# A 17-tap convolution in a graph kernel, computed through Fourier components along the nodes

## The chip, the cores and the metric

One core of one Trainium2 chip runs the whole program. The metric is the device time of one execution in microseconds (us), the median of several. "Clock" is the share of full speed that the throttle granted to TensorE. A ratio is the mean time of one kernel's fast runs over the mean time of the other's fast runs of the same rounds, so it is not quite the ratio of the medians quoted beside it.

## The reference, cut to what matters

128 graphs of 128 nodes with 256 channels, in float32. Layer 0 is a gated update whose input comes from a convolution along the nodes and from a weighted sum over neighbours. Layer 1 is a small graph convolution on the first 25 nodes.

```python
def _L0_gnn_ref(x, mask, w_se, b_se, conv1_w, ..., conv2_w, ...):
    xc = jnp.transpose(x, (0, 2, 1))
    h = _bn(_conv1d(xc, conv1_w, 0), bn1_g, bn1_b, bn1_m, bn1_v)
    h = jax.nn.relu(h)
    h = _bn(_conv1d(h, conv2_w, 8), bn2_g, bn2_b, bn2_m, bn2_v)   # 17 taps, 256 -> 256 channels
    x_conv = jnp.transpose(jax.nn.relu(h + xc), (0, 2, 1))
    ...                                    # x_nmp: exp(-dist) * mask times relu(x @ w_msg.T)
    x_in = jnp.concatenate([x_conv, x_nmp], axis=-1)
    gi = x_in @ w_ih.T + b_ih
    gh = x @ w_hh.T + b_hh
    ...                                    # gates r, z, n
    return (1.0 - z) * nn_ + z * x
```

## The kernel before

The graphs go through in 32 passes of four (4 x 128 nodes = 512 columns). Everything stays in SBUF: a pass normalises, transposes and applies the first convolution (`front`), computes the 17-tap convolution (`conv2`), the neighbour sum and the gates (`gru`). After every four passes one block of layer 1 is interleaved with the next passes (`block`).

```python
    def conv2(q, between):
        xc = fr.tile([P, 2, 512], FP, tag="xc", name=f"xc{q}")
        src = h1p[q % 2]                                   # [128, 2, 4 graphs, 128 + 16 nodes]
        for co in range(2):
            pc = pacc.tile([P, 512], FP, tag="acc", name=f"p2{q}_{co}")
            i = 0
            for k in range(2):
                for t in range(TAPS):
                    nc.tensor.matmul(pc.rearrange("p (j n) -> p j n", j=GB),
                                     c2w[:, k, t, co * P:(co + 1) * P], src[:, k, :, t:t + N],
                                     start=(i == 0), stop=(i == 2 * TAPS - 1))
                    i += 1
            ...                                            # batch norm, residual, relu
            if co == 0:
                between()                                  # a piece of layer 1, then neighbours(q)
        return xc
    # ... cut ...
    for q in range(NQ):
        xc = conv2(q, between)
        if q + 1 < NQ:
            front(q + 1)
        gru(q, xc)
        # ... loads, and block(q // QS) after every fourth pass
```

## Time and profile before

| before | value | how to read it |
|---|---|---|
| time | 3819.15 us (3818.87 to 3821.99, 3 runs) | the spread is 0.1% |
| matmuls of `conv2` | 2176 of 512 columns, 1911 us busy of the 3674 us of TensorE | half of the kernel |
| DMA | 57 MB, 15 GB/s in the mean | the queues are busy in the first slice alone |

The prediction shows the lines that carry this. Two more lines of the page matter for the comparison: TensorE's granted clock in 40 slices of the span, in tenths, and the DMA total.

```profile
PEclk9999999999999999999999999999999999999996
DMA packets 62287, 56.84 MB, mean 15 GB/s; under 512 B 7381, under 2 KB 59738, under 8 KB 61914
```

TensorE runs at full clock everywhere but in the last slice, and the memory system is idle.

### The profile page before, as it was taken

The page shows a single profiled execution, that of the slowest core. Times are in us where ns is not written, and L with a number is a line of the kernel's source. Part 1 is how long each engine was busy: PE and PEld are TensorE (multiplying, and loading weights), DVE is VectorE, ACT ScalarE, POOL GpSimd, SP SyncE. Part 2 cuts the span into 40 slices and gives each one's busy share as a digit, 9 for nine tenths or more (in the row PEclk, how much of TensorE's full clock was granted, in tenths as well). Part 3 has the DMA queues.
Part 4 walks back from the last instruction along what each step waited for, and adds up shares of the span by engine and source line. Part 5 has one row for each costly group of instructions (what it writes and reads, how often), then busy time and mean ns, then how long its engine had stood idle before and what let it go on. Part 6 is the DMA issues. An engine that isn't in the chain of part 4 may idle for free.

```text
span 3818.0 us, 25995 instructions
## 1 busy us (share of the span) xinstructions
PE 3673.6 (96%) x10930; PEld 1828.5 (48%) x10930; DVE 605.0 (16%) x1370; ACT 544.2 (14%) x833; POOL 392.2 (10%) x536
## 2 busy tenths in 40 slices
PE   5999999999999999999999999999999999999997
PEld 2444445544445544555445554445544455444454
DVE  1111121111111111111211112111121111211112
ACT  0111110111111111111111111111111111111111
POOL 1010010101101011000110001000010100110000
PEclk9999999999999999999999999999999999999996
DMA  4000000000000000000000000000000000000000
GB/s 155 10 13 13 3 13 13 13 10 18 4 13 13 13 15 12 4 13 13 16 13 3 13 13 18 10 13 3 13 18 13 10 7 9 19 13 10 7 5 11
DMA packets 62287, 56.84 MB, mean 15 GB/s; under 512 B 7381, under 2 KB 59738, under 8 KB 61914
## 3 DMA queue, kind: packets, MB, share of 16 engines
q1 hardware_dynamic: 55808, 41.97, 4.1%
q10 hardware_dynamic: 6362, 13.22, 1.0%
q8 instruction: 85, 1.39, 0.1%
q14 instruction: 32, 0.26, 0.0%
HBM read 38.38 MB, written 16.78 MB: 14 GB/s over the span
## 4 chain that ended last, share of the span: by engine, by line
PE 94%; POOL 2%; ACT 1%; DMA 1%; DVE 1%; issue 0%; ACTq 0%; POOLq 0%; SPq 0%; DVEq 0%
PE p L316 47%; PE pz L342 9%; PE pr L342 9%; PE pn L342 6%; PE pc L250 3%; PE pm L295 3%; PE pg L342 3%; PE ph L452 3%; PE pz L458 3%; PE px L303 2%; PE pse L259 1%; POOL d L363 1%; POOL go L365 1%; PE pg L477 1%; PE pd L273 1%; PE po L378 1%
## 5 line engine op out<-in xcount | busy, mean ns | idle before, releaser
L316 PE MATMUL p<-h1p,c2w 128*128 128x512 f32 x4352 | 1911.1, 592 | 0.0
L316 PEld LDWEIGHTS p<-h1p,c2w 128*128 128x128 f32 x4352 | 809.8, 188 | 962.1 <-issue 956.8
L362 POOL TENSOR_TENSOR d<-hT,r 128x512 f32<-128x512 f32 x64 | 82.5, 1288 | 2014.7 <-ACT r L355 2014.7
L320 DVE SCALAR_TENSOR_TENSOR xc<-p,s_bn,hT 128x512 f32<-128x512 f32 x64 | 48.1, 751 | 1228.7 <-PE p L316 1228.7
L243 ACT ACTIVATE hT<-ph 128x512 f32<-128x512 f32 x64 | 37.9, 592 | 794.4 <-PE ph L241 794.4
L454 ACT ACTIVATE hh<-ph,vec 128x96 f32<-128x96 f32 (+3 forms) x160 | 61.9, 399 | 556.6 <-PE ph L452 551.5
L351 DVE SCALAR_TENSOR_TENSOR r<-pg,vec,r 128x512 f32<-128x512 f32 x64 | 48.0, 751 | 544.5 <-PE pg L342 503.9
L250 PE MATMUL pc<-hT,c1w 128*128 128x512 f32 x256 | 120.2, 613 | 7.7 <-ACT hT L243 7.7
L285 POOL TENSOR_TENSOR b<-adj,cst 25x12 f32<-25x12 f32 (+4 forms) x256 | 52.5, 235 | 671.8 <-DMA adj<-in_adj 556.7
L295 PE MATMUL pm<-wmsg,hT 128*128 128x256 f32 x512 | 121.1, 379 | 0.0
L322 ACT ACTIVATE xc<-xc,t_bn 128x512 f32<-128x512 f32 x64 | 45.8, 716 | 526.4 <-DVE xc L320 526.4
L342 PE MATMUL pr<-hT,whh 128*128 128x512 f32 x256 | 120.3, 592 | 0.0
L342 PE MATMUL pz<-hT,whh 128*128 128x512 f32 x256 | 120.3, 592 | 0.0
L342 PE MATMUL pz<-xnmp,wih 128*128 128x512 f32 x256 | 120.3, 592 | 0.0
L342 PE MATMUL pg<-hT,whh 128*128 128x512 f32 x256 | 120.3, 592 | 0.0
L342 PE MATMUL pz<-xc,wih 128*128 128x512 f32 x256 | 120.3, 592 | 0.0
L342 PE MATMUL pn<-xnmp,wih 128*128 128x512 f32 x256 | 120.3, 592 | 0.0
L342 PE MATMUL pr<-xnmp,wih 128*128 128x512 f32 x256 | 120.3, 592 | 0.0
L342 PE MATMUL pn<-xc,wih 128*128 128x512 f32 x256 | 120.3, 592 | 0.0
L342 PE MATMUL pr<-xc,wih 128*128 128x512 f32 x256 | 120.3, 592 | 0.0
L452 PE MATMUL ph<-yz,w 128*128 128x96 f32 (+3 forms) x640 | 109.0, 323 | 0.5 <-DVE yz L444 0.5
L458 PE MATMUL pz<-hh,w 128*128 128x96 f32 (+3 forms) x640 | 108.3, 322 | 0.0
(121 smaller groups left out, 2663.2 us busy)
## 6 DMA issues: line engine op xcount, KB each, us to landing
xt<-in_x SPq DMA_DIRECT2D x128, 128.0 KB, 2.7
out<-xt SPq DMA_DIRECT2D x128, 96.0 KB, 1.9
adj<-in_adj SPq DMA_DIRECT2D x32, 256.0 KB, 2.8
w<-in_W ACTq DMA_DIRECT2D x2, 2560.0 KB, 15.6
c2w<-in_conv_w ACTq DMA_DIRECT2D x2, 2176.0 KB, 12.9
out<-x SPq DMA_DIRECT2D x128, 32.0 KB, 1.6
wih<-in_w_ih ACTq DMA_DIRECT2D x1, 1536.0 KB, 11.2
whh<-in_w_hh ACTq DMA_DIRECT2D x1, 768.0 KB, 13.7
```

The source lines that it names most:

```text
L250: nc.tensor.matmul(pc, c1w[:, k, co * P:(co + 1) * P], hT[:, k], start=(k == 0), stop=(k == 1))
L285: nc.gpsimd.tensor_tensor(b1[:, b0:b0 + GB, r:r + w], ad[:NN, :, n:n + w], ident[:NN, None, n:n + w].to_broadcast([NN, GB, w]), ALU.add)
L295: nc.tensor.matmul(pm[:, i], hT[:, k, j * N:(j + 1) * N], wmsg[:, k], start=(k == 0), stop=(k == 1))
L303: nc.tensor.matmul(px[:, dc, i], msg[:, i, dc * P:(dc + 1) * P], aT[:, 2 * h + i], start=True, stop=True)
L316: nc.tensor.matmul(pc.rearrange("p (j n) -> p j n", j=GB), c2w[:, k, t, co * P:(co + 1) * P], src[:, k, :, t:t + N], start=(i == 0), stop= ...
L320: nc.vector.scalar_tensor_tensor(xc[:, co], pc, scl["bn2"][:, co:co + 1], HT[q][:, co], op0=ALU.mult, op1=ALU.add)
L342: nc.tensor.matmul(ps, w, a, start=(i == 0), stop=(i == len(ops) - 1))
L351: nc.vector.scalar_tensor_tensor(r, ph, v("b_hh", 4 + dc), r, op0=ALU.add, op1=ALU.mult)
L362: nc.gpsimd.tensor_sub(d, hT[:, dc], r)
L452: nc.tensor.matmul(ph, w1[:, g, k, m * P:(m + 1) * P], yz[:, k, :, o:o + n], start=(k == 0), stop=(k == 1))
L454: nc.scalar.activation(hh[:, m], ph, AF.Relu, bias=v("b1", g * 4 + m))
L458: nc.tensor.matmul(pz, w2[:, g, m, cc * P:(cc + 1) * P], hh[:, m], start=(m == 0), stop=(m == 3))
```

## The change

A convolution along the nodes is a product, component by component, in a Fourier basis along the nodes. With length 136 = 128 + 8 the wrapped ends don't reach the nodes that are kept. 17 multiply passes become a forward transform, one complex product for each component and an inverse transform. A component's product needs all graphs at once to fill TensorE (128 graphs are the rows of its output), so the work becomes three stages with DRAM between them. Stage 1 is 32 passes of `front` and neighbours, each with its forward transform; among them stand eight chunks that transform the taps and store them (`wd`). Stage 2 multiplies component by component. Stage 3 is the inverse transform, the gates and layer 1. The core of the diff, with cuts:

```diff
-    def conv2(q, between):
-        ...                                   # 68 matmuls of 512 columns in a pass
+    def first_stage(es):
+        ...                                   # front(q), back(q): as before, outputs stored to DRAM
+            for k in range(2):                # forward transform of a pass
+                pf = p2.tile([P, 2, 2 * D], FP, tag="b2", name=f"pf{q}_{k}")
+                for h in range(2):
+                    for i in range(2):
+                        nc.tensor.matmul(pf[:, h, i * NC:(i + 1) * NC],
+                                         H1[q, h][:, i, k * P:(k + 1) * P], c("fh"), ...)
+        TC = 8
+        def taps(ch):
+            wt = fa.tile([P, TC, D], FP, tag="wt", name=f"wt{ch}")
+            for i in range(4):                # 17 taps in each of four groups of 32 rows
+                nc.sync.dma_start(out=wt[i * 32:i * 32 + 16], in_=src[:16])
+                nc.sync.dma_start(out=wt[i * 32 + 16:i * 32 + TAPS], in_=src[16:])
+            for j in range(TC // 2):
+                for i in range(4):            # 16 products: 17 rows, 128 components, 512 columns
+                    pw = p1.tile([P, 512], FP, tag="t", name=f"pw{ch}_{j}_{i}")
+                    nc.tensor.matmul(pw, fw[i * 32:i * 32 + TAPS, :P], rows(i, j), ...)
+                    ws = fa.tile([P, 512], FP, tag="ws", name=f"ws{ch}_{j}_{i}", bufs=3)
+                    ...                       # ScalarE or VectorE: ws <- pw
+                    nc.sync.dma_start(out=wd[:P, ...], in_=ws)              # 256 KB
+            for i in range(4):                # 16 narrow products: the other 8 components
+                pw = p1.tile([P, 512], FP, tag="t", name=f"pwt{ch}_{i}")
+                for j in range(TC // 2):
+                    nc.tensor.matmul(pw[j * WIDE:(j + 1) * WIDE],
+                                     fw[i * 32:i * 32 + TAPS, P:P + WIDE], rows(i, j), ...)
+                ...                           # ws (tag "wst", one buffer) <- pw, four small stores
+        for q in range(NQ):
+            ...                               # front(q), back(q - 1)
+            if q % 3 == 1 and q // 3 < n_chunks:
+                taps(q // 3)
+    def second_stage(es):
+        for b in range(NC // 4):              # 34 blocks of four components
+            wt = sb.tile([P, 4, 2 * D], FP, tag="wt", name=f"wf{b}", bufs=3)
+            nc.sync.dma_start(out=wt, in_=wd[4 * b:4 * b + 4]...)           # 1 MB
+            ...                               # wm = wi - wr, wp = wr + wi; xs = xr + xi
+            ...                               # k1 = xs wr, k2 = xr wm, k3 = xi wp: 12 matmuls of 256
+            nc.vector.tensor_add(yy[:, :, 1], s, ks[1])
+            nc.vector.tensor_sub(yy[:, :, 0], s, ks[2])
+            nc.scalar.dma_start(out=to, in_=yt)                             # 0.5 MB
+    def inverse(q):                           # stage 3: 2 matmuls of 512, 8 of 128 columns
+        ...
```

## The prediction

> **What bounds the kernel now.** I read the page first (busy shares, slices), then the chain that ended last, then the groups of instructions kept apart by shape, and last the timeline of one pass and of the tail.
>
> ```profile
> PE 3673.6 (96%) x10930; PEld 1828.5 (48%) x10930; DVE 605.0 (16%) x1370; ACT 544.2 (14%) x833; POOL 392.2 (10%) x536
> PE   5999999999999999999999999999999999999997
> DMA  4000000000000000000000000000000000000000
> ```
>
> TensorE works without a gap from the second slice on, the other engines are at 16% or less, and the DMA queues matter in the first slice alone. So TensorE's columns are the time. Groups and chain say which:
>
> ```profile
> L316 PE MATMUL p<-h1p,c2w 128*128 128x512 f32 x4352 | 1911.1, 592 | 0.0
> L342 PE MATMUL pr<-hT,whh 128*128 128x512 f32 x256 | 120.3, 592 | 0.0
> L303 PE MATMUL px<-aT,msg 128*128 128x128 f32 x512 | 69.5, 279 | 0.0
> L483 PE MATMUL pf<-zt,s2w 128*64 128x256 f32 x128 | 24.6, 468 | 12.5 <-ACT zt L480 12.5
> ...
> 162.23 27.55 PE p L316 x64
> 199.91 25.83 PE p L316 x60
> 267.63 27.55 PE p L316 x64
> ```
>
> L316, the 17-tap convolution, has 4352 records for 2176 matmuls, two records each. 64 records take 27.55 us, so a record takes 430.5 ns and a matmul of 512 columns 861 ns: 1.68 ns a column. One group of four graphs (a pass; 32 of them) holds 68 such matmuls, 58.5 us; from 162.23 to 267.63 a pass without layer 1 takes 105.4 us. The durations that I use below come from the timeline:
>
> ```profile
> 1398.53 0.87 PE L378 MATMUL po<-cst,go 128*128 128x128 f32 x6 [1.54 <-POOL go L365]
> 1402.35 0.65 PE L483 MATMUL pf<-zt,s2w 128*64 128x256 f32 x4
> 1446.84 1.06 PE L273 MATMUL pd<-rt,lt 67*128 67x128 f32 x8
> 1448.17 1.89 PE L295 MATMUL pm<-wmsg,hT 128*128 128x256 f32 x8
> 1452.49 1.05 PE L303 MATMUL px<-aT,msg 128*128 128x128 f32 x8
> ...
> 3718.89 1.12 PE L483 MATMUL pf<-zt,s2w 128*64 128x256 f32 x4 [1.94 <-ACT zt L480]
> ```
>
> The last record of a run ends about 0.16 us late (592 less 430 ns), so I take that off: a matmul of 256 columns 0.43 us, of 128 columns 0.22 us (67 rows cost what 128 rows cost), a transpose, a single record, 0.11 us.
>
> **What the Trainium skill says.** "FP8 and Floating Point Precision", TensorE Precision Notes: true FP32 takes four passes through the array. The trace agrees: 4 x 512 columns at 2.4 GHz are 853 ns, and I read 861. "TensorE: Matmul & The Clock Gate", Part 3 (Packing small matmuls): matmuls in different 32-row or 32-column groups of the array run at the same time. For columns the trace agrees: the pair at 1402.35 takes 0.49 us without its tail, where two 256-column matmuls in turn take 0.86. For rows nothing here shows it. Same page, Part 1: the array's clock halves after a window of some 3.4 us with little work. The trace agrees in the tail: the same pair takes 1.12 us at 3718.89, and the windows give half clock there.
>
> ```profile
> core 0: us, PE busy (x) PEld busy (x) DVE busy (x) ACT busy (x) POOL busy (x), PEclk, DMA share, GB/s
> 3722.00:3740.00 18.00, 11.96 (x35) 6.20 (x36) 3.34 (x6) 3.08 (x5) 2.63 (x1) 0.50 0.08 22
> ...
> 30.00:40.00 10.00, 0.00 (x0) 0.00 (x0) 1.93 (x9) 0.00 (x0) 1.01 (x1) 1.00 1.06 364
> ```
>
> "DMA: Bandwidth & Descriptors", Latency and other measured facts: rows at a pitch of a large power of two are slow (512 KiB: 207 GB/s). The new stores have pitches of 256 KiB (transformed taps) and 128 KiB (products). No transfer of this trace has them; its loads reach 364 GB/s.
>
> **The change part by part.** It removes 2176 matmuls of 512 columns: 2176 x 0.861 = 1874 us. It adds on TensorE:
> - forward transform, 8 matmuls of 136 columns a pass: 8 x 136 x 1.68 ns = 1.84 us, x32 = 59 us;
> - transform of the taps, eight chunks of 16 + 16 matmuls of 512 columns on 17 rows: 8 x 32 x 0.861 = 220 us in turn, less where they run side by side;
> - products, 33 x 12 + 10 = 406 matmuls of 256 columns: 406 x 0.43 = 175 us;
> - inverse, 8 of 128 and 2 of 512 columns a pass: 1.76 + 1.72 = 3.5 us, x32 = 111 us.
>
> That is at most 565 us for 1874 us. But the convolution was also the filler behind which everything else hid, and the work is now three stages with a barrier between them. So I sum by stage, from the instruction orders of the built program.
>
> Stage 1, one pass: 8 transposes 0.87, 8 matmuls of 512 columns 6.9, w_se 1.72, distances 0.88, adjacency 0.44, messages 1.76, transform 1.84: 14.4 us. DVE has some 10.8 us a pass (layernorm 4.1, two adds of 1024 elements 2.4, w_se 1.5, copies and mask 2.8), so TensorE still leads, but its order has short waits: for hT (0.4 us, as now), for ScalarE's copy between the two transform tiles that share a PSUM buffer (1.0), for the four operations behind w_se (DVE 0.74 + 0.73, then ACT 0.68 + 0.68; 0.5 left open), and for copies that free PSUM before the next transposes (0.7). 17 us x32 = 544 us, and 15 us for the first loads.
>
> Taps: each of a chunk's 16 products is copied (0.6 to 0.7 us) into one of three buffers and stored, 256 KB. A 96 KB store lands in 1.9 us; for 256 KB at the pitch above I estimate 3 us, with issue and copy 4 us, over three buffers 1.3 us each: 21 us. The 16 narrow ones run in four column groups, about 4 us, and their single staging buffer waits for four stores a time, which I give 3 us beyond what hides: 28 us x 8 = 224 us. Whether rows run side by side does not matter, since the stores pace it.
>
> Stage 2: a block needs TensorE 12 x 0.43 = 5.2 us. DVE has four operations, 2 x 1.23 (1024 elements, from 0.42 at 256 and 0.69 at 512) + 2 x 0.69 = 3.8 us, ordered two blocks ahead. DMA moves 1 MB in and 0.5 MB out: 4.1 us at 364 GB/s, 5.5 if the stores run at half rate. I take 6 us x 34 = 204 us, and 10 us to fill, since the first load waits for the end of stage 1.
>
> Stage 3, one pass: 36 gate matmuls 31.0, transposes 0.87, inverse 3.0 (its two row groups partly together), waits 2.5 (1.54 for go as now, the rest for layer 1): 37.4 us x 32 = 1197 us. The loads of a pass (2.1 MB, 6 us) are issued one pass ahead in the queue's order, so they hide. Layer 1 stays: 3818 less the start 45, the tail 106 (after the last gate) and 32 x 105.4 leaves 294 us; plus that same tail, 106. Entering stage 3, constants, gate and layer-1 weights and two passes' inputs, 12 MB, take about 34 us, of which 10 us are worked: 25 us lost.
>
> Sum: 15 + 544 + 224 + 214 + 1197 + 294 + 106 + 25 = 2619 us. I say 2610.
>
> **The rivals.**
> - DRAM becomes the bound of stage 2. For it: 1.5 MB a block, and the pitch. Against it: 364 GB/s in the loads of now. At 9 us a block stage 2 costs 100 us more: 2720.
> - Half clock. Stage 2 and the tap chunks leave TensorE with gaps, and the tail shows that some 55% busy is enough to drop it. In the chunks it costs little (the stores pace them) but each later pass starts slow, some 5 us x 8; if stage 1's passes stayed at half clock they would be dense, and dense work restores it, as the tail's clock shows from 3763 on. 2650 to 2700.
> - The removed filler comes back as waits: layer 1 and the gate's end used to be padded with convolution. The built order still pads layer 1 with gate matmuls, one or two at a place, as before, so I give it no more than 1 us a pass. At 5 us a pass: 2740.
> - The taps cost less: if stores run at full rate and all groups side by side, a chunk takes 15 us, and stage 1 a pass of 15.5 us: 2460.
> - No gain at all would need 1200 us of waits; none of the above comes near.
>
> **Range and chances.** Stage 3 is mostly counted columns and is good to some 40 us. Stages 1 and 2 carry the doubt: taps -90/+100, passes -50/+60, products -25/+100. Not all go one way: 2490 to 2760. Faster by over 2% is nearly certain (0.97); 0.02 within; 0.01 slower.
>
> **What will show it.** Stage 1's passes without taps at 17 us, with TensorE 85% busy; tap chunks near 28 us in which TensorE waits for ACT and DVE, and these for stores of ws; a stage 2 block at 5.2 to 6 us with the wait of k1 on a load small; passes of stage 3 at 37 us without and 47 with layer 1; two loads of ScalarE's tables where 64 were. I am wrong if k1 waits for loads in every block, if DVE sets stage 1's pass (over 85% busy), or if the granted clock falls below 0.95 outside start, chunks and tail.

## The result, and the profile after

The changed kernel takes 2656.32 us (2655.43 to 2667.21, 4 runs) against 3819.01 us (3818.62 to 3821.99, 4 runs) of the kernel before in the same rounds: ratio 0.6961, 95% interval 0.6942 to 0.6979. The predicted 2610 us is 46 us (1.7%) short, and the range of 2490 to 2760 holds the result. All outputs are right. First the page of the changed kernel: busy times, then slices of the span, then the DMA total.

```profile
PE 2377.4 (90%) x8806; PEld 1357.3 (51%) x8806; DVE 824.3 (31%) x1625; ACT 529.3 (20%) x854; POOL 403.6 (15%) x377
...
PE   7888888888887997998999999999999999999977
...
PEclk8877789877999998999999999999999999999977
DMA  4344343433325987221122121121121221220100
...
DMA packets 170661, 249.43 MB, mean 94 GB/s; under 512 B 21165, under 2 KB 112818, under 8 KB 170546
```

TensorE lost 1296 us of busy time and is still the engine that is busy all along, but no longer evenly. Slices 1 to 12 (stage 1) show 7 to 9 tenths, and their clock is below 9 in most: that is new. Slices 14 and 15 (stage 2) are those in which DMA is nearly full, and slice 16 holds the entry of stage 3 with its loads. After it the picture is that of before. The stages stand apart on the timeline; here are the ends that tell them (start, length, operation, idle time before it and what ended it):

```profile
819.46 0.86 PE L321 MATMUL pf<-cst,h 128*128 128x136 f32 x6
830.96 3.75 PE L404 MATMUL pr<-wf,xh 128*128 128x256 f32 x8 [10.64 <-DMA wf<-wd]
```

```profile
837.22 1.89 PE L424 MATMUL k<-wf,xs 128*128 128x256 f32 x8
...
842.40 1.89 PE L424 MATMUL k<-wf,xs 128*128 128x256 f32 x8
```

```profile
1006.43 1.89 PE L424 MATMUL k<-wp,xh 128*128 128x256 f32 x8
...
1023.69 2.56 PE L517 MATMUL pi<-cst,yl 32*128 32x512 f32 x4 [15.36 <-DMA yl<-ytd]
```

So stage 1 ends at 820.3 us, stage 2 lasts from 831.0 to 1008.3, a block of it 842.40 - 837.22 = 5.2 us, and stage 3 takes the rest, with two waits at the seams, 10.64 and 15.36 us. Beside the prediction:

| part | predicted | measured | difference |
|---|---|---|---|
| stage 1: start, 32 passes, 8 tap chunks | 15 + 544 + 224 = 783 | 820.3 | +37 |
| seam to stage 2 | 10 | 10.6 | +1 |
| stage 2, 34 blocks | 204 | 177.3 | -27 |
| stage 3 with entry and tail | 25 + 1197 + 294 + 106 = 1622 | 1647.0 | +25 |
| sum | 2619 | 2655.3 | +36 |

A pass of stage 1 that has no chunk near it, from the first line to the last:

```profile
586.99 0.60 PE L258 MATMUL ph<-cst,xt 128*128 128x128 f32 x4
...
588.34 7.13 PE L271 MATMUL pc<-cm,hT 128*128 128x512 f32 x16
595.30 1.88 PE L281 MATMUL pse<-hT,wse 128*67 128x512 f32 x4
...
604.30 0.87 PE L258 MATMUL ph<-cst,xt 128*128 128x128 f32 x6 [0.69 <-ACT aT L293]
```

It takes 17.3 us (predicted 17.0). The chunk that stands before the previous pass is where the argument lies:

```profile
539.98 1.95 PE L349 MATMUL pw<-wt,cst 17*128 17x512 f32 x4 [0.69 <-ACT aT L293]
546.65 13.28 PE L349 MATMUL pw<-wt,cst 17*128 17x512 f32 x28 [4.72 <-DMA wt<-in_conv_w]
559.86 1.96 PE L362 MATMUL pwt<-wt,cst 17*32 17x512 f32 x16
562.51 2.42 PE L362 MATMUL pwt<-wt,cst 17*32 17x512 f32 x16 [0.69 <-ACT wst L367]
564.85 1.11 PE L258 MATMUL ph<-cst,xt 128*128 128x128 f32 x4
```

From 540.0 to 564.9 it lasts 24.9 us; two products start, TensorE waits 4.72 us for the chunk's taps, and 14 products (28 records) take 13.28 us. The last line, the next pass, starts slowly: four transposes take 1.11 us where they take 0.60 at 586.99. The windows tell why. Columns are the stretch, its length, busy time of TensorE, its weight loads, VectorE, ScalarE and GpSimd with instruction counts, then clock, DMA share, GB/s:

```profile
540.00:545.00 5.00, 1.93 (x4) 0.56 (x4) 3.52 (x9) 1.61 (x2) 1.01 (x1) 0.96 0.46 149
...
555.00:560.00 5.00, 5.00 (x17) 2.10 (x24) 2.08 (x3) 1.19 (x2) 0.00 (x0) 0.50 0.70 263
560.00:565.00 5.00, 4.31 (x33) 0.62 (x31) 0.69 (x1) 1.08 (x2) 0.00 (x0) 0.50 0.42 155
565.00:570.00 5.00, 4.31 (x11) 2.44 (x12) 0.69 (x1) 1.20 (x2) 0.00 (x0) 0.50 0.26 91
...
575.00:580.00 5.00, 4.41 (x17) 2.09 (x15) 1.40 (x2) 1.72 (x3) 0.00 (x0) 1.00 0.15 39
```

TensorE works without a gap from 555 to 560 and yet has half clock. It keeps it to 571.9. That is the larger part of why the pass after a chunk takes 22.1 us in place of 17.3; the other part, 2.0 us, is a wait of that pass for VectorE's copy of the neighbour sum (`xm` <- `px`), which the free pass above does not have:

```profile
586.03 1.13 PE L311 MATMUL px<-aT,h 128*128 128x128 f32 x8 [2.00 <-DVE xm L313]
```

Cut at the steps of the clock, the windows show one stretch at half clock behind each chunk's start:

```profile
544.62:571.92 27.30, 23.75 (x74) 9.61 (x75) 5.62 (x9) 5.87 (x10) 0.00 (x0) 0.50 0.54 188
571.92:626.53 54.61, 44.79 (x208) 27.47 (x206) 29.74 (x65) 17.22 (x24) 3.02 (x3) 1.00 0.32 100
```

These two lengths, 27.3 us at half clock and 54.6 at full clock, repeat from the first chunk to the eighth.

Three passes and one chunk repeat; I call that a cycle and read its length from the starts of the second and the eighth chunk, 130.6 and 621.8: 491.2 / 6 = 81.9 us. Three free passes would be 3 x 17.3 = 51.9, so a chunk costs 30 us with what it does to its neighbour. The cycle is the measure of the experiments below; eight of them make up most of stage 1.

In stage 3 the gates are as predicted; the transposes behind them wait longer. One place of many:

```profile
1292.93 1.54 PE L580 MATMUL po<-cst,go 128*128 128x128 f32 x6 [2.31 <-POOL go L567]
```

And the tail is the tail of before, to the hundredth of a microsecond in this line:

```profile
2556.05 1.12 PE L692 MATMUL pf<-zt,s2w 128*64 128x256 f32 x4 [1.94 <-ACT zt L689]
```

### The profile page after: what moved, and what is told of

It is laid out like the page before. It is cut to its first block, busy times and chain, and to the rows that moved or that the text cites. A ratio compares the mean times of both kernels' runs of the same rounds, so it can differ in the third digit from the quotient of the medians.

```text
span 2655.3 us, 23745 instructions
## 1 busy us (share of the span) xinstructions
PE 2377.4 (90%) x8806; PEld 1357.3 (51%) x8806; DVE 824.3 (31%) x1625; ACT 529.3 (20%) x854; POOL 403.6 (15%) x377
## 5 line engine op out<-in xcount | busy, mean ns | idle before, releaser
L271 PE MATMUL pc<-cm,hT 128*128 128x512 f32 x512 | 248.9, 642 | 6.4 <-ACT hT L260 6.4
L564 POOL TENSOR_TENSOR d<-hTl,r 128x512 f32<-128x512 f32 x64 | 81.0, 1265 | 855.9 <-issue 602.3
L271 PEld LDWEIGHTS pc<-cm,hT 128*128 128x128 f32 x512 | 102.5, 207 | 132.5 <-issue 107.9
L349 PE MATMUL pw<-wt,cst 17*128 17x512 f32 x256 | 119.8, 1068 | 43.7 <-DMA wt<-in_conv_w 36.7
L544 PE MATMUL pr<-hTl,whh 128*128 128x512 f32 x256 | 122.4, 597 | 0.0
L544 PE MATMUL pg<-hTl,whh 128*128 128x512 f32 x256 | 122.3, 595 | 0.0
L544 PE MATMUL pn<-xml,wih 128*128 128x512 f32 x256 | 121.9, 594 | 0.0
L544 PE MATMUL pz<-xml,wih 128*128 128x512 f32 x256 | 121.4, 592 | 0.0
L544 PE MATMUL pr<-xml,wih 128*128 128x512 f32 x256 | 121.3, 592 | 0.0
L544 PE MATMUL pz<-hTl,whh 128*128 128x512 f32 x256 | 120.3, 592 | 0.0
```

Of the source, the lines that this page charges most:

```text
L271: nc.tensor.matmul(pc[:, i], hT[:, k, j * N:(j + 1) * N], cm[:, k], start=(k == 0), stop=(k == 1))
L349: nc.tensor.matmul(pw, fw[i * 32:i * 32 + TAPS, :P], rows(i, j), start=True, stop=True)
L544: nc.tensor.matmul(ps, w, a, start=(i == 0), stop=(i == len(ops) - 1))
L564: nc.gpsimd.tensor_sub(d, hT[:, dc], r)
```

## The experiments

Two theories stood at the start. The prediction's own: a chunk is paced by its 4 MB of stores through three buffers. The rival, from the windows above: it is paced by TensorE at half clock, because only 17 of 128 rows work, and by the late request for the taps. Stage 2 had its own pair: TensorE's columns, or DMA close behind.

### Six buffers in place of three

```diff
-  ws = fa.tile([P, 512], FP, tag="ws", name=f"ws{ch}_{j}_{i}", bufs=3)
+  ws = fa.tile([P, 512], FP, tag="ws", name=f"ws{ch}_{j}_{i}", bufs=6)
```

> The copies of the transformed taps get six buffers in place of three; nothing else changes. Theory of the prediction (a tap chunk is paced by its 4 MB of stores through three buffers): a chunk falls from 25 to about 18 us, eight of them by about 55 us, and the whole from 2656 to about 2600 us. Rival (a chunk is paced by TensorE, which runs at half clock there, and by the wait for the taps' own load): a chunk stays within 1.5 us of 25 and the whole within 12 us of 2656; the product groups in a chunk are as long as before.

Measured: 2608.57 us (2601.63 to 2611.33), ratio 0.6827; the cycle is 75.1 us. The chunk on the timeline of this run:

```profile
501.75 2.21 PE L349 MATMUL pw<-wt,cst 17*128 17x512 f32 x4 [0.69 <-ACT aT L293]
506.98 11.81 PE L349 MATMUL pw<-wt,cst 17*128 17x512 f32 x28 [3.02 <-DMA wt<-in_conv_w]
518.72 2.79 PE L362 MATMUL pwt<-wt,cst 17*32 17x512 f32 x32
```

The chunk falls from 24.9 to 19.7 us, close to the 18 of the prediction's theory, and the rival as I put it has fallen: the buffers do hold it up. But most of the gain is not in the products (13.28 to 11.81 us). It is spread over the wait for the taps, the narrow products, and the next pass (22.1 to 19.9, where the 2.0 us wait for VectorE's copy is gone), and the products are still slow. Neither theory is enough.

### Every store twice

```diff
+  nc.sync.dma_start(out=wd2[:P, ...], in_=ws)     # a scratch area; same source
```

> Each 256 KB of transformed taps is stored twice, the second time to a scratch area: 33.5 MB more. Theory of the prediction (paced by stores): a chunk grows from 25 to about 40 us or more, the whole by about 100 us or more. Rival (TensorE at half clock): the stores have room, a chunk grows by under 5 us and the whole by under 40 us, unless doubling pushes the stores over the limit; then a chunk would last about 8 MB at the best rate seen in this trace (291 GB/s), 29 us, and the whole +30 us.

Measured: 2707.94 us (2696.51 to 2711.39), ratio 0.708; the cycle is 87.7 us, a chunk 29.4 to 30.5 us. It adds 52 us where pacing by stores asked for 100 or more, and where ample room asked for under 40. The chunk has the length of the rival's second branch (29 us), the whole lies between the two theories. In the chunk at 573.5 the copies wait 21.6 us in all for the stores, in the one at 540.0 of the changed kernel 1.6 us. So in the changed kernel the stores are near the limit, not at it.

### The taps requested a pass earlier

```diff
+  if q % 3 == 1 and q // 3 < n_chunks:
+      load_taps(q // 3)                            # the eight loads, out of taps()
   now = front(q)
```

> The taps of a chunk are requested before the front of the pass that precedes the chunk, not at the chunk itself; same tiles, same work. Theory (each chunk loses 4.7 us because its taps are requested only when it starts): the wait of the products for the taps goes, a chunk falls from 25 to about 20.5 us, and the whole falls by 8 x 4.7 = 38 us to about 2618 us. Rival (the wait only fills time that the half clock takes anyway, or the load delays the pass's own loads): under 10 us gained.

Measured: 2633.46 us (2630.40 to 2636.04), ratio 0.6894; the cycle is 78.6 us. A chunk of this run:

```profile
444.08 3.86 PE L354 MATMUL pw<-wt,cst 17*128 17x512 f32 x14 [0.69 <-ACT aT L293]
451.37 9.22 PE L354 MATMUL pw<-wt,cst 17*128 17x512 f32 x18 [3.43 <-DVE ws L360]
460.52 4.58 PE L367 MATMUL pwt<-wt,cst 17*32 17x512 f32 x32
```

The wait for the taps is gone, and 3.3 of its 4.7 us come out of the cycle. The first seven products take 3.86 us: 0.55 us each, before the clock falls; the nine after it take 1.02 us each. Now the wait of 3.43 us is for the copies, which wait for the stores. So one wait had hidden the other.

### Both together

```diff
   (the edits of the two runs: six buffers, and the early request)
```

> Six store buffers and the early request together. Theory (two separate losses in a chunk, the wait for a free store buffer and the wait for the taps): the gains add up or do a little better, since with the taps there the buffers are what is waited for: the chunk about 15 us (sum of the single steps: 24.9 - 5.2 - 4.0), the whole 2656 - 47 - 23 = 2586 us or a little less, and no wait for taps or stores of over 1 us left in a chunk. Rival (TensorE at half clock sets a floor of 16 x 0.95 + 4 = 19 us): the whole stays near 2605 us.

Measured: 2620.54 us (2618.25 to 2622.95), ratio 0.6861; the cycle is 76.8 us. This is 12 us worse than six buffers alone. The chunk is indeed shorter, 18.7 us, but the next pass is back at 22.5 us:

```profile
509.20:527.90 18.70, 16.55 (x64) 5.45 (x64) 9.89 (x24) 6.43 (x10) 1.01 (x1) 0.59 0.68 256
527.90:550.40 22.50, 18.19 (x79) 11.22 (x76) 7.99 (x14) 6.48 (x9) 0.00 (x0) 0.88 0.24 70
550.40:567.70 17.30, 16.37 (x71) 10.15 (x69) 7.01 (x15) 4.23 (x6) 1.01 (x1) 0.91 0.30 101
```

With both waits reduced the clock of the chunk is 0.59 all the same, and some of the loss has moved to the passes after it. One part of that is a plain wait: the 2.0 us for VectorE's copy, which six buffers alone had taken away but for once, are back behind every chunk, and this cycle is 1.7 us longer than theirs. What brings the wait back no run shows. For the chunk the rival's floor at half clock fits (19 us, measured 18.7). And this run shows that TensorE need not stand idle for the clock to fall. Here are the 3.4 us before the step and after it:

```profile
509.16:512.57 3.41, 3.32 (x14) 1.83 (x14) 2.61 (x5) 2.57 (x5) 0.00 (x0) 1.00 0.28 114
512.57:515.98 3.41, 3.41 (x11) 1.50 (x8) 2.77 (x11) 1.31 (x3) 0.47 (x1) 0.50 1.00 381
```

By the profile, which models the ends of matmuls, TensorE is busy with the chunk's products for 3.32 of 3.41 us, and then the clock is halved. The next runs take the half clock away.

### All 128 rows in every product

```diff
+  fwm = fa.tile([P, 4, P + WIDE], FP, name="fwm")   # per group: its 17 rows of fw, zeros elsewhere
-  nc.tensor.matmul(pw, fw[i * 32:i * 32 + TAPS, :P], rows(i, j), ...)
+  nc.tensor.matmul(pw, fwm[:, i, :P], wt[:, 2 * j:2 * j + 2], ...)  # and the narrow ones alike
```

> Each product of the tap transform uses all 128 rows, with zeros in the rows of the other three groups: the same columns and results, but no two products side by side. Theory (the clock falls because only 17 rows work in a chunk): the clock in a chunk rises from 0.59 to over 0.8 and the pass after a chunk takes about 17.5 us in place of 21.9; a product then costs its full 0.86 us, a chunk is about 16 x 0.86 + 14 + 4.7 = 32 us, and the whole is about 2656 + 8 x (7 - 4.4) = 2677 us. Rival (the clock falls because of the waits in a chunk, whatever the rows): clock 0.6 as before, the pass after it 22 us, and a chunk of over 45 us, the whole over 2800 us.

Measured: 2661.70 us (2659.80 to 2664.20), ratio 0.6971; the cycle is 82.1 us. As expected, two things trade. The wait for the taps grew to 7.9 us, since no product can start before all groups have landed, and each product costs its full 0.86 us; but the clock in the chunk is 0.90, not 0.59, despite that longer wait, and the next pass takes 19.8 us. About 17.5 had been expected there; 2.0 us of the difference are the wait for VectorE's copy, which is there in this run too:

```profile
550.20:569.60 19.40, 19.38 (x64) 7.57 (x64) 5.54 (x8) 5.26 (x9) 0.00 (x0) 0.90 0.53 202
569.60:589.40 19.80, 16.18 (x76) 10.20 (x73) 6.46 (x8) 5.78 (x8) 0.00 (x0) 0.97 0.32 99
```

That is the decisive pair with the window 555 to 560 above: the same columns, the same results, TensorE busy in both; the rows at work differ (and with them whether products run side by side, which no run separates from the rows), and so does the clock. The half clock that is left begins at 547.1, during the wait for the taps, and ends at 554.0, 3.8 us after the products start.

### The chunks spread over all passes, with 17 rows and with 128

The taps are cut into 32 pieces, one for each pass, four products and four narrow ones, placed in twos among the pass's matmuls and requested a pass ahead; the store buffers are four, and the narrow products share one copy. The second run fills the rows as above.

```diff
-  TC = 8                       # taps(ch) as one stretch after every third pass
+  TC = 2                       # taps(q) is a generator; front and back call next() at three places
```

> The transform of the taps is cut into 32 small pieces, one for each pass, requested a pass ahead, and its matmuls are placed in twos among the pass's other matmuls; the same 128 products and 128 short products. Theory (TensorE's clock falls to half because a chunk keeps only 17 rows at work for 25 us, which costs in the chunk and in the pass after it): the clock of stage 1 stays near 1, the added time is about 32 x 4 us in place of 8 x (25 + 4.7), so the whole falls by about 80 to 110 us to about 2560 us. Rival (the products cost about the same wherever they stand; a matmul of 17 rows among others overlaps nothing and takes its 0.86 us): 32 x 8 us, the whole within 25 us of 2656.

> The spread version again, with zero rows filled up to 128 in each product. In the spread version a pass took 30.7 us at a clock of 0.77, in place of 17.3. Theory (a few matmuls of 17 rows in a pass are enough to lower the clock): with full rows the clock is above 0.95 and a pass takes about 17.3 + 8 x 0.86 = 24 us, the whole about 2797 - 32 x 6.5 = 2590 us. Rival (rows do not count; the short waits and small matmuls of a longer pass lower the clock): clock near 0.77 and 2797 us or more.

Measured: 2797.00 us (2795.23 to 2800.05), ratio 0.7324, with 17 rows; 2674.07 us (2661.66 to 2688.66), ratio 0.7003, with 128. One window of stage 1 for each, first the run with 17 rows:

```profile
200.00:960.00 760.00, 645.30 (x2216) 334.36 (x2214) 282.23 (x591) 176.36 (x249) 24.48 (x25) 0.78 0.31 101
```

```profile
200.00:820.00 620.00, 520.68 (x2051) 291.68 (x2048) 263.66 (x555) 164.86 (x234) 23.18 (x23) 0.89 0.36 117
```

My theory missed both. I had thought that thin matmuls between thick ones would keep the clock; instead 17 rows in a few places of every pass gave 0.78 in all of stage 1, a pass of 30.7 us, and the worst time of all. Filling the rows gains 123 us, so the rows count here too, but a pass still takes about 26.5 us in the mean, not 24, at a clock of 0.89. What lowers the clock there besides the rows is open; a wait of 3.0 us in each pass (for VectorE's copy of the neighbour sum) and the run of short matmuls around it are candidates that no run separates.

### Four direct products in stage 2

```diff
-  k1 = xs wr, k2 = xr wm, k3 = xi wp            # 12 matmuls of 256 columns in a block
+  re = xr wr - xi wi, im = xr wi + xi wr        # 16; no wm, wp on VectorE
```

> Stage 2 multiplies each pair of components with four products in place of three: 16 matmul pairs of 256 columns in a block in place of 12, without the two additions of weights on VectorE; the same bytes. Theory (stage 2 is bound by TensorE, 100% busy at 5.2 us a block): 5.2 x 16/12 = 6.9 us a block, stage 2 177 -> 235 us, the whole +57 us to about 2713 us. Rival (TensorE only seems busy and the transfers, 85% busy, or VectorE set the pace): 5.2 to 5.7 us a block, the whole within 15 us of 2656.

Measured: 2719.37 us (2716.07 to 2722.30), ratio 0.712: +63 us. Stage 2 of the changed kernel, then of this run:

```profile
830.90:1008.20 177.30, 177.24 (x812) 155.56 (x812) 119.39 (x135) 20.71 (x35) 41.80 (x32) 0.99 0.85 291
828.50:1063.00 234.50, 234.49 (x1078) 206.17 (x1079) 22.56 (x33) 20.68 (x35) 47.65 (x32) 0.99 0.71 220
```

234.5 us / 34 = 6.9 us a block, 16/12 of 5.2, while VectorE's work fell from 119 to 23 us. So the columns of TensorE set the pace of stage 2. It grew by 57 of the 63 us.

### Half of the loads of stage 2 twice

```diff
+  w2x = sb.tile([P, 2, 2 * D], FP, tag="w2x", name=f"w2x{b}", bufs=2)
+  nc.sync.dma_start(out=w2x, in_=wd[4 * b:4 * b + 2]...)      # nobody reads it
```

> In stage 2 each block loads half of its weights a second time into a tile that nobody reads: 1.5 MB in and 0.5 MB out in place of 1 and 0.5. Theory (TensorE sets the pace of stage 2 and DMA, 85% busy at 291 GB/s, is a close second): 2 MB at the 374 to 420 GB/s that the entry of stage 3 shows is 4.8 to 5.4 us, but at this mix of loads and stores the 85% says at most 342 GB/s, 5.9 us a block, so DMA becomes the bound: 5.6 to 6.2 us a block, the whole +14 to +34 us. Rival (ample room): 5.2 us a block and within 8 us of 2656.

Measured: 2668.22 us (2655.49 to 2671.05), ratio 0.6979, 95% interval 0.6965 to 0.6993: +12 us in the medians, which is not clear of the spread, since the interval of the changed kernel reaches 0.6979 too. The profiled run was the shortest, 2655.49 us, but only because its stage 1 ended at 815.5, 4.8 us sooner; its stage 2 takes 183.3 us (826.1 to 1009.4) against 177.4. In it:

```profile
828.00:1008.00 180.00, 174.98 (x804) 152.72 (x803) 126.21 (x133) 20.70 (x35) 44.34 (x32) 1.00 1.00 381
```

```profile
PE k L427 <- DMA wf<-wd: 5.0, 4, 1.5
```

DMA is at 1.00 of its time and 381 GB/s, and the products wait for loads four times, 5.0 us in all. A block takes 5.4 us, where the theory asked for 5.6 to 6.2 and the rival for 5.2. The truth lies between the two: a third more bytes cost 6 us of stage 2, and then the engines are busy all the time. The 85% of the kernel as it stands did not mean that 15% were left: the same engines moved 31% more bytes a second.

### All remedies in one, with six buffers and with three

Early request, products on 128 rows, six buffers, and one thing more: the narrow products of all four groups as one matmul with a block-diagonal weight, which fills the rows without wasting them. Their copy also takes its buffer from the six (or three) now and no longer has a single one.

```diff
-  for i in range(4):                            # 16 narrow matmuls, 4 copies in a chunk
-      for j in range(TC // 2): nc.tensor.matmul(pw[j * WIDE:(j + 1) * WIDE], fw[...], rows(i, j), ...)
+  for j in range(TC // 2):                      # 4 matmuls, 1 copy: 4 groups x 8 components = 32
+      nc.tensor.matmul(pw[j * WIDE:(j + 1) * WIDE], fwt, rows(j), start=True, stop=True)
```

> All remedies in one: taps requested a pass ahead, products on 128 rows with zeros (no half clock), the narrow products of all four groups as one matmul with a block-diagonal weight (4 matmuls and one copy in a chunk in place of 16 and 4), six store buffers. Theory (a chunk is 16 x 0.86 us of products at full clock plus some 2 us, and the pass after it keeps its clock): chunk about 16.5 us, the next pass 17.3 to 18.5 us, 8 x (24.9 + 4.7 - 16.5 - 1) = 97 us less, the whole about 2560 us. Rival (the stores, 4 MB in 16 us at 255 GB/s beside the pass's own transfers, hold it up, or the clock falls all the same as in the six-and-early run): 2600 us or more.

> The same with three store buffers. Theory (at full clock a product comes each 0.86 us, faster than three buffers of 256 KB are emptied, which took about 1.3 us each with the taps early): a chunk grows from about 16.5 to 20 us, the waits of the copies for the stores are back, the whole about 28 us above the run with six. Rival (three buffers are enough once TensorE's clock is up): within 8 us of the run with six.

Measured: 2562.33 us (2560.69 to 2567.87, 5 runs), ratio 0.6712, 95% interval 0.6703 to 0.6721, with six buffers; 2579.52 us (2570.13 to 2579.79), ratio 0.6747, with three. With six, a chunk on the timeline, then its window and those of the two passes after it:

```profile
466.48 9.71 PE L360 MATMUL pw<-wt,fwm 128*128 128x512 f32 x22 [0.69 <-ACT aT L293]
477.71 4.56 PE L360 MATMUL pw<-wt,fwm 128*128 128x512 f32 x10 [1.52 <-DVE ws L366]
482.20 1.07 PE L372 MATMUL pwt<-wt,fwt 128*32 128x512 f32 x8
```

```profile
466.50:483.20 16.70, 15.18 (x41) 6.06 (x41) 10.01 (x24) 5.78 (x9) 1.01 (x1) 1.00 0.66 249
483.20:500.50 17.30, 15.44 (x76) 9.62 (x72) 5.58 (x7) 4.74 (x8) 0.00 (x0) 1.00 0.43 125
500.50:518.00 17.50, 15.45 (x72) 9.63 (x72) 9.38 (x22) 5.64 (x8) 1.01 (x1) 1.00 0.36 111
```

This came out as expected: chunk 16.7 us, the next pass 17.3, the clock 1.00 throughout, the cycle 69.1 us. With three buffers the cycle is 70.9 and a chunk 17.2 to 17.8 us, where 20 was expected: the buffers still matter, but 17 us in the whole, less than the 28 that I had expected. The products give up running side by side and are still quicker, since 0.86 us at full clock is less than the 0.95 (13.28 / 14) that two or so at a time took at half clock.

### The weights behind the inputs at the entry of stage 3

```diff
-  whh = weight(wp, w_hh, ..., nc.scalar)         # and wih, w1, w2: ScalarE's DMA queue
+  whh = weight(wp, w_hh, ..., nc.sync)           # SyncE's, behind the loads of the first pass
```

> The version with all remedies, and at the entry of stage 3 the gate and layer-1 weights move from ScalarE's DMA queue to SyncE's, behind the first pass's own inputs; the 64 KB of products (yl) then no longer lie behind 2.3 MB of gate weights. Theory (the 15.4 us wait for yl at the entry is the last store of stage 2 and this small load standing behind the weights): the wait falls to about 6 us, the whole by 8 to 10 us from 2562 to about 2553 us (ratio to before about 0.669 against 0.671). Rival (what is waited for is the 4.6 MB that the entry needs anyway): the wait moves to the gate weights, and the whole stays within 3 us of 2562.

Measured, on top of the version above: 2556.18 us (2552.35 to 2558.29, 5 runs), ratio 0.6692, 95% interval 0.6683 to 0.6702. That is 6 us, somewhat less than the 8 to 10 expected, and the runs of the two versions don't overlap. TensorE's waits at this seam, first without the move, then with it (total us, times, longest):

```profile
PE pi L526 <- DMA yl<-ytd: 20.4, 2, 15.5
```

```profile
PE pb L505 <- DMA b2s<-in_b: 9.2, 1, 9.2
PE pi L526 <- DMA yl<-ytd: 5.6, 2, 4.6
```

The wait for `yl` fell as foreseen, and 9.2 of the 14.8 us that it gave went to a 5 KB bias (`b2s`) for a matmul that now came first in TensorE's order. It is the fastest version here, 100 us (3.8%) below the changed kernel.

### What the cycles have in common

Every cycle above is the difference of two chunk starts, over six cycles. The clock's share of it is worked out from the mean clock c of the same stretch as 2 x (1 - c) x cycle (the steps shown above are between 1.00 and 0.50), with c rounded to hundredths, so good to about 1 us. The last column divides the cycle by the Trainium skill's window of 3.413 us (its page is named in the last section).

| version | cycle, us | mean clock | at half clock, us | cycle in windows |
|---|---|---|---|---|
| the changed kernel | 81.9 | 0.83 | 28 | 24.0 |
| six buffers | 75.1 | 0.86 | 21 | 22.0 |
| stores twice | 87.7 | 0.81 | 33 | 25.7 |
| early taps | 78.6 | 0.84 | 25 | 23.0 |
| six and early | 76.8 | 0.85 | 23 | 22.5 |
| full rows | 82.1 | 0.94 | 10 | 24.0 |
| all remedies, three buffers | 70.9 | 0.99 | 1 | 20.8 |
| all remedies | 69.1 | 1.00 | 0 | 20.2 |

Where the clock falls, most cycles are a whole or a half number of windows; the spread version's pass of 30.7 us is nine of them. Where it doesn't fall, they are not. The steps of the clock show it without a mean: in the changed kernel 27.3 and 54.6 us are 8 and 16 windows, with six buffers each cycle has 20.5 us at half clock and 54.6 at full clock, 6 and 16, and with early taps all cycles but one have 23.9 and 54.6, 7 and 16. So a saving of a few microseconds in a throttled cycle shows in steps: the early request gave one window, six buffers two, both together one and a half. That fits all of these but the doubled stores. It would explain why two remedies did worse than one, but so would the 2.0 us wait for VectorE's copy that came back with both. That the lock is the cause is argued from these numbers, and no run shifted the phase by itself.

## Why the prediction was right, point by point

- **The sum by stages.** Right in size, and the time is in the range. The removed 1874 us were counted from the columns, and so was most of what was added; those parts came out within a few per cent.
- **Stage 1's passes, 17.0 us.** Right: 17.3 us with TensorE at 89% (15.4 of 17.3). Only the pass behind each chunk (22.1) and the last passes (17.5 to 20.0) are longer. The half-clock rival had this to its credit, "each later pass starts slow, some 5 us x 8": it was 4.8, though 2.0 of that was the wait for VectorE's copy and only the other 2.8 can be the clock's.
- **The tap chunks, 28 us.** The size is near (24.9 us, and 30 with the slow pass behind), but the cause was wrong. The steps that failed read "Whether rows run side by side does not matter, since the stores pace it" and, of half clock in the chunks, "it costs little (the stores pace them)". The runs show three causes that hide each other: the late request for the taps, the three buffers, and a clock of 0.50 while 17 rows work. The 2.0 us wait for VectorE's copy in the next pass comes and goes with them. Taking away the first two one at a time gave 3.3 and 6.8 us of the cycle, both together 5.1, all three with the block-diagonal narrow products 12.8. The stores alone, with full clock, are worth 1.8 (three buffers against six).
- **Stage 2, 6 us a block.** Mechanism right ("5.2 to 6 us"), size too careful: 5.2 us. I had put 0.8 us a block on top of TensorE's columns for DMA and got none of it. (The 4.1 us for a block's transfers are 1.5 MB at 364 GB/s; 1024 and 512 KB are 1.57 MB, 4.3 us.) The rival of slow stores at the large pitch did not come: the stage moved 291 GB/s, and 381 with more loads. The direct products scaled by 16/12, as a TensorE bound asks.
- **The seam to stage 2, 10 us.** Right: 10.64.
- **Stage 3.** The entry lost 15.36 + 3.77 = 19 us to the two waits for `yl`, where I gave 25. The tail lasted 106 us, as before. What is between took 1647 - 19 - 106 = 1522 us, where my terms give 1197 + 294 = 1491: 31 us more. The largest term that was mis-sized is the wait for the gates' result: in all 65.2 us before the transposes, 2.04 a pass, where I took the 1.54 of one place in the profile before; that makes 16 of the 31. The rest is not assigned.
- **What would have proved me wrong** did not come about, but for one line: "if the granted clock falls below 0.95 outside start, chunks and tail". It did, behind every chunk. Of the signs it named, the two table loads in place of 64 came, and stage 3's first three passes, without layer 1, took 37.1 to 39.4 us (37 was said).

## What to carry to other kernels

Count the columns of each stage, and then ask of every stretch with few rows what clock TensorE will get there and just after it; padding the rows with zeros can be faster than running thin matmuls side by side. When several waits end close together, removing one shows the next, and removing two may even lose, so try them together with the cause that is left. At a seam between stages, look at what stands ahead of the first small load in the queues.

## What the Trainium skill lacked or had wrong

- "TensorE: Matmul & The Clock Gate", Part 1 (The HAM clock gate) tells the clock by how busy TensorE has been and warns of idle gaps. Lacking: the rows that work count too, or the running side by side that came with few rows. TensorE was busy 5.00 of 5.00 us with products on 17 rows at a clock of 0.50; the same products on 128 rows had 0.90 behind a wait of 7.9 us, and 1.00 without that wait; and with the taps there in time the clock fell after 3.41 us of which TensorE was busy 3.32. Its window of 3.413 us agrees with the trace, where stretches of 27.3, 23.9 and 20.5 us at half clock are 8, 7 and 6 of it. What it doesn't say is that a throttled loop can settle at a whole number of windows: 81.9 us is 24, 75.1 is 22, 30.7 is 9.
- The same page, Part 3 (Packing small matmuls) gives 3.07 times for four row groups at 512 columns. For FP32 products of 17 rows, each with its own weight and output of 128 columns, the runs show less: 0.55 us each at full clock (7 in 3.86 us) where one alone takes 0.861, 1.6 times; at half clock 0.95 against twice that one, 1.72, 1.8 times. At half clock the copies have a part in it: behind the wait at 546.65 four products start within 1.7 us and end at 549.39, 2.5 times as fast as one after the other, and the fifth starts at 549.38, when the first copy out of PSUM has just ended (549.33). What holds it at full clock no run shows.
- No page that I read says how far a DMA share below 1 is from the limit; "Perfetto Trace Analysis", Identifying the Most-Contended Engine, warns that the occupancy of the 16 DMA engines misleads, and gives no number. In stage 2 a share of 0.85 went with 291 GB/s and a share of 1.00 with 381: 31% more bytes for 18% more share.
